# A GpSimd add behind each of 736 gathers in a four-layer sparse graph network

## The chip, the cores and the metric

The kernel runs on one core of a Trainium2 chip. The metric is device time in microseconds (us). Engines: PE is TensorE (matrix products; PEld its weight loads), DVE is VectorE, ACT is ScalarE, POOL is GpSimd, SP is SyncE, which only issues transfers here.

## What is computed

Four graph layers over 4096 nodes with 128 features each and one 4096x4096 weighted adjacency matrix, of which only a small part is not zero. Every layer normalises the rows, applies relu and adds its result to x:

```python
# layer 0
h = relu(layernorm(x)); x = x + h @ W_self.T + (adj @ h) @ W_neigh.T + b
# layer 1: three Chebyshev terms
h = relu(layernorm(x)); T1 = adj @ h; T2 = 2 * (adj @ T1) - h
x = x + h @ w[0] + T1 @ w[1] + T2 @ w[2] + bias
# layer 2: attention over the edges
H = h @ weight.T; C = alpha_src[None, :] + alpha_dst[:, None]
Tau = adj.T * exp(max(0.2 * C, C)); att = Tau / sum(Tau, axis=1)
x = x + (adj.T * att) @ H
# layer 3: one message for each edge
s = h @ msg_s; d = h @ msg_d
agg[i] = sum_j gelu(s[i] + d[j] + msg_b) * adj[i, j]
f = gelu(concat(h, agg) @ upd_w.T + upd_b) + h; x = x + layernorm(f)
```

The nodes are put in another order before the launch, so that nodes with many edges come first.

## The kernel before

The matrix is read once, half a block of 128 rows at a time (1 MB each), and turned into flags: ACT makes a mask of what is not zero (L768), DVE reduces it by columns (L783) and packs it into words (L788, L790), of which it takes the largest eight of each segment (L797). From the flags come lists. For each of 16 stripes of 256 rows, and likewise of columns, a list says which far rows of a block have an entry in the stripe at all; blocks near the diagonal and dense ones are taken whole. The lists are made in `pairs` (L627 to L675: small DVE instructions, and PE products with a selection matrix from `selection`, L619). For layer 3 every single edge is listed (`entries`, L805), 128 to a chunk, 158 chunks in all.

All that is listed is fetched by gathers: one indirect transfer on POOL's queue for 128 rows, by an index tile. They are issued by the helper `gather` (L552), so all have the line L553. By what they write and read:

- `rseg<-in_adjT` (68) and `cseg<-in_adj` (74): 256-column pieces of far matrix rows for the row and the column stripes. SP stores them in the tables `r_tab` and `c_tab` in HBM (L722), from which later layers read them as whole tiles `big`.
- `g<-h_tab` (136) and `g<-u_tab` (68): rows of the normalised features for layer 0 and for the first product of layer 1 (`h_tab`), and of layer 1's intermediate result for its second product (`u_tab`) (L1120).
- `g<-a_tab` (74): the same for attention (L1212).
- `e_val<-in_adj` (158): the matrix value of each edge (L937).
- `<-d_tab` (158): the rows d[j] of layer 3 (L1351), into tiles that the profile calls m, e or tau, as they share memory with attention's tiles of these names.

Other work on POOL: at the start tables of indices and constants, then xN + b0 for eight blocks at a time (L979, four of 128x1024), xN + b1 for four blocks (L1000, eight of 128x512), and four memsets (L1592). `pause` does not exist yet; `ones` (L445) is a 128x128 tile of ones that stays unchanged after L446.

The order on every engine is written by a planner in the kernel itself (class `Plan`, L255). Each piece of work is a generator that yields an engine with a planned duration, an event, or a pool of buffers; the planner always lets the piece start that can start earliest, and among those that could start at almost the same time the one with the lowest rank. A gather is planned with `GATHER`, 1.27 us on POOL. The value gathers (`values`, rank 6) and column pieces (rank 4) yield to the layers (rank 0). The result is kept: `in_order` (L348) ties each instruction to its predecessor on its engine. So each engine works through one fixed queue, and an instruction that waits holds up all behind it.

If PE has a planned gap of more than 0.8 us, `fill` (L604) puts products with a tile of zeros into it, one for each 0.22 us of 80% of the gap, into a free PSUM bank.

The Tile framework adds the waits on semaphores. A gather waits for its index tile, for the last reader of its buffer, and for the landing of the gather eight before it.

Of the kernel before, what the change touches and what calls it, by code (L numbers as in the profile page):

```python
# [27 lines left out]
P = 128  # L28
# [344 lines left out]


SP = "SP", 0.07
GATHER = "POOL", 1.27


def sparse_stack(tc, x, adj, adjT, diag, w_self, w_neigh, b0, w1, b1, w2, att_src, att_dst,
# [7 lines left out]
    nc = tc.nc  # L387
    plan = Plan()
    EARLY = 7
    with ExitStack() as ctx:  # L390
# [4 lines left out]
        def tiles(pool, name, n, shape, dtype=F32):  # L395
            return Slots([pool.tile(list(shape), dtype, name=f"{name}{i}", tag=f"{name}{i}") for i in range(n)])

        def kept(name, shape, dtype=F32):
            return keep.tile(list(shape), dtype, name=name, tag=name)
# [17 lines left out]
        banks = tiles(ps, "bank", 3, (P, BANK))  # L417
        picks = tiles(ps, "pick", 2, (P, BANK))
# [26 lines left out]
        ones = kept("ones", (P, P))  # L445
# [103 lines left out]
        junks = tiles(keep, "junk", 2, (P, D))  # L549
        aggs = tiles(keep, "agg", 2, (P, BANK))  # L550

        def gather(dst, table, index):  # L552
            nc.gpsimd.indirect_dma_start(out=dst, out_offset=None, in_=table[:, :],  # L553
                                         in_offset=bass.IndirectOffsetOnAxis(ap=index, axis=0))


        def norm(blocks, dst):
# [45 lines left out]

        def fill(begin, time):  # L604

            idle = min((free, i, slots.items) for slots in (banks, picks) for free, i in slots.free + [(1e9, 0)])
            if idle[0] < begin - 1.0:
                for _ in range(int(time / 0.22)):
                    nc.tensor.matmul(idle[2][idle[1]], nothing[:, :P], nothing, start=True, stop=True)  # L609
# [121 lines left out]
        def fetch_columns():  # L731
            for s in COLS:
                if s.cap:
                    yield col_list[s.index]
                for k in range(s.cap):
                    t = yield csegs
                    yield GATHER
                    gather(t, adj_segments, seg_col[:, s.chunk + k:s.chunk + k + 1])
                    here, left = Event(), Count(1)
                    here.set(plan.transfer(P * CS * 4))  # L740
                    plan.start(store(here, t, csegs, left, c_tab[s.index][k * P:(k + 1) * P, :], c_done[s.index],
                                     P * CS * 4), 6)
                    plan.start(give_back(left, csegs, t), 0)
# [186 lines left out]
        def values():  # L930
            for number, group in enumerate(GROUPS):
                yield decoded[number]
                for u in group.units:
                    for k in range(u.chunk, u.chunk + u.cap):
                        yield GATHER
                        n = u.within(k)
                        gather(e_val[:n, k:k + 1], adj_flat, e_at[:n, k:k + 1])  # L937
                        valued[u.number].set(plan.finish + plan.LANDING)
                    plan.start(valid(u), 7)
# [125 lines left out]
        class Layer:  # L1065
# [36 lines left out]
            def gather(self):  # L1102
                for s in ROWS:
                    if s.cap:
                        yield row_list[s.index]
                    for c in range(s.cap):
                        if self.number == 0:
                            t = yield rsegs
                            yield GATHER
                            gather(t, adjT_segments, seg_row[:, s.chunk + c:s.chunk + c + 1])  # L1110
                            here, left = Event(), Count(2)
                            here.set(plan.transfer(P * RS * 4))
                            self.at["seg", s.index, c] = t, here, left
                            plan.start(store(here, t, rsegs, left, r_tab[s.index][c * P:(c + 1) * P, :],
                                             r_done[s.index], P * RS * 4), 2)
                            plan.start(give_back(left, rsegs, t), 0)
                        g = yield rows_g
                        yield self.table_done
                        yield GATHER
                        gather(g[:, :D], self.table, fetch_row[:, s.chunk + c:s.chunk + c + 1])  # L1120
                        self.at["row", s.index, c] = g
                        self.rows_here[s.index][c].set(plan.transfer(P * D * 4))
# [51 lines left out]
        class Attention:  # L1174
# [33 lines left out]
            def rows(self, s, chunks, rows):  # L1208
                yield a_table
                for c, (g, here) in zip(chunks, rows):  # L1210
                    yield GATHER
                    gather(g, a_tab, fetch_col[:, s.chunk + c:s.chunk + c + 1])  # L1212
# [103 lines left out]
        class Messages:  # L1316
# [27 lines left out]
            def rows(self, u, chunks, m, here):  # L1344
# [3 lines left out]
                for q, k in enumerate(chunks):  # L1348
                    yield GATHER
                    n = u.within(k)  # L1350
# [300 lines left out]
def gnn_stack_kernel(tc, **args):  # L1651


    some_bad = sparse_stack(tc, **args)
    with tc.If(some_bad > 0):
        args.pop("diag")
        dense_stack(tc, **args)
# [329 lines left out]
```

## Time and profile before

| what | value |
|---|---|
| median of 9 runs | 1197.01 us (1193.78 to 1200.44) |
| the profiled execution, timed | 1198.3 us |
| its span, from first to last instruction | 1196.4 us |
| busy: PE / DVE / ACT / POOL | 988.1 / 797.7 / 673.1 / 769.3 us |
| mean granted PE clock | 0.921 |
| moved by DMA | 236.03 MB, mean 197 GB/s |
| e_val<-in_adj gathers | 158, mean 1011 ns |
| g<-h_tab gathers | 136, mean 980 ns |
| g<-a_tab gathers | 74, mean 1047 ns |
| zero products of fill (L609) | 795, 532 of them with mean 407 ns |
| chain that ended last | DMA 21%, PE 20%, DVE 12%, POOL 10%, issue 8%, ACT 6% |

The profile comes from one execution. Busy time counts instructions that an engine carries out; waiting, branches and the issue of plain transfers do not count. A gather counts as busy while POOL makes its descriptors, not while the data travel. Where one row of the profile joins several instructions, its duration runs from the first start to the last end. "issue" is time in which an engine waited for nothing that the profile shows.

Stages of this execution: reading, scanning, lists and layer 0 up to about 345 us; the rest of the column pieces, both products of layer 1, the features for attention and the decoding of the edges up to about 720; attention up to about 965; messages and the end up to 1196.

### The profile page before, as it was taken

To read this page: it belongs to the slowest core of one execution; us is meant where nothing else is said; L and a number is where in the kernel's file an instruction comes from. 1 tells how busy PE (TensorE), PEld (TensorE's weight loads), DVE (VectorE), ACT (ScalarE), POOL (GpSimd) and SP (SyncE) were. 2 spreads that over 40 slices of the span, in tenths; PEclk is the share of its full clock that TensorE was granted. 3 is DMA by queue.
4 is the path that set the end of the run, shared out by engine and by line. 5 is a ranking of instruction groups with operands and counts; after the bars stand their busy time and mean duration, and the time that the engine had idled before them with its cause. 6 is when DMAs were issued, how large, how long until landed. Compare 5 with 4: busy or idle time off the path is not lost.

```text
span 1196.4 us, 19187 instructions
## 1 busy us (share of the span) xinstructions
PE 988.1 (83%) x5943; PEld 678.6 (57%) x5943; DVE 797.7 (67%) x2982; ACT 673.1 (56%) x1344; POOL 769.3 (64%) x832
## 2 busy tenths in 40 slices
PE   5878989888888888878879798989999997879860
PEld 2545666555546666657767554454555655657650
DVE  5789988798788858758768575455555733456652
ACT  4997666677423121323456485676778632545771
POOL 5115777355466767777777777777777747777710
PEclk9988889888889999989999899999999999999985
DMA  7999999999659778899767433444445222233300
GB/s 225 372 329 346 387 390 395 373 334 374 197 159 301 217 217 272 272 269 277 226 177 211 136 89 111 115 113 115 115 127 144 68 59 53 51 75 79 78 22 21
DMA packets 175415, 236.03 MB, mean 197 GB/s; under 512 B 22452, under 2 KB 155336, under 8 KB 167112
## 3 DMA queue, kind: packets, MB, share of 16 engines
q1 hardware_dynamic: 148904, 186.45, 46.3%
q0 software_dynamic: 26400, 48.27, 16.1%
q8 instruction: 49, 0.80, 0.3%
q14 instruction: 62, 0.51, 0.1%
HBM read 203.41 MB, written 31.23 MB: 196 GB/s over the span
## 4 chain that ended last, share of the span: by engine, by line
DMA 21%; PE 20%; DVE 12%; POOL 10%; issue 8%; ACT 6%; SPq 0%; POOLq 0%; ACTq 0%; DVEq 0%
POOL e_val L553 4%; DMA e_val<-in_adj,e_at 4%; PE acc L1138 3%; DMA cseg<-in_adj,seg_col 3%; POOL g L553 3%; DMA g<-h_tab,fetch_row 3%; PE acc L1155 2%; DMA tau<-d_tab,e_col 2%; PE acc L1254 2%; PE acc L1252 2%; DMA g<-a_tab,fetch_col 2%; DMA big<-in_adjT 2%; DMA m<-d_tab,e_col 2%; DMA big<-r_tab 2%; PE bank L597 2%
## 5 line engine op out<-in xcount | busy, mean ns | idle before, releaser
L553 POOL DMA_INDIRECT e_val<-in_adj,e_at x158 | 159.7, 1011 | 48.0 <-issue 40.7
L553 POOL DMA_INDIRECT g<-h_tab,fetch_row x136 | 133.3, 980 | 44.7 <-issue 26.4
L609 PE MATMUL pick<-nothing 128*128 128x512 f16 x532 | 137.8, 407 | 0.0
L609 PEld LDWEIGHTS <-nothing 128*128 128x128 f16 x795 | 81.6, 105 | 90.8 <-issue 22.3
L1138 PE MATMUL acc<-big,hA 128*128 128x256 f32 x448 | 120.7, 415 | 6.9 <-DMA big<-in_adjT 4.8
L553 POOL DMA_INDIRECT rseg<-in_adjT,seg_row x68 | 70.0, 1030 | 75.0 <-issue 22.8
L1138 PEld LDWEIGHTS acc<-big,hA 128*128 128x128 f32 x448 | 89.2, 208 | 21.5 <-DMA big<-in_adjT 6.0
L553 POOL DMA_INDIRECT cseg<-in_adj,seg_col x74 | 71.4, 965 | 39.2 <-issue 20.5
L768 ACT ACTIVATE mask<-dst 128x2048 fp8e4<-128x2048 f32 x43 | 81.9, 1904 | 24.2 <-DMA dst<-in_adj 24.1
L553 POOL DMA_INDIRECT g<-a_tab,fetch_col x74 | 77.5, 1047 | 22.6 <-issue 14.6
L1155 PE MATMUL acc<-big,g 128*128 128x256 f32 x272 | 78.0, 421 | 16.4 <-DMA big<-r_tab 10.1
L553 POOL DMA_INDIRECT m<-d_tab,e_col x70 | 68.3, 975 | 21.3 <-issue 12.8
L553 POOL DMA_INDIRECT tau<-d_tab,e_col x63 | 61.2, 972 | 30.1 <-issue 11.6
L1235 DVE TENSOR_TENSOR tau<-e,big 128x512 f32<-128x512 f32 (+3 forms) x61 | 54.3, 890 | 39.3 <-ACT e L1231 37.1
L553 POOL DMA_INDIRECT g<-u_tab,fetch_row x68 | 64.9, 955 | 20.7 <-issue 10.1
L568 ACT ACTIVATE junk<-xN,stat 128x128 f32<-128x128 f32 x128 | 51.3, 401 | 40.0 <-DVE stat L564 29.5
L887 ACT COPY ehit<-pick 128x192 f32<-128x192 f32 (+7 forms) x74 | 20.3, 287 | 89.6 <-PE pick L884 70.7
L1155 PEld LDWEIGHTS acc<-big,g 128*128 128x128 f32 x272 | 52.8, 208 | 28.5 <-DMA g<-h_tab,fetch_row 10.4
L609 PE MATMUL bank<-nothing 128*128 128x512 f16 x263 | 68.3, 402 | 0.0
L1138 PE MATMUL acc<-big,hB 128*128 128x256 f32 x224 | 59.5, 403 | 7.7 <-DMA big<-in_adjT 7.7
L890 DVE SCALAR_TENSOR_TENSOR ehit<-ehit,pos,pick 128x32 f32<-128x32 f32 (+7 forms) x158 | 38.7, 284 | 38.0 <-ACT ehit L887 37.7
L622 ACT ACTIVATE sel_t<-iota_row,mids 128x512 f32<-128x512 f32 (+3 forms) x43 | 27.1, 642 | 57.7 <-DVE mids L617 55.7
(328 smaller groups left out, 2612.9 us busy)
## 6 DMA issues: line engine op xcount, KB each, us to landing
dst<-in_adj SPq DMA_DIRECT2D x43, 1024.0 KB, 9.6
big<-in_adjT SPq DMA_DIRECT2D x45, 512.0 KB, 7.3
raw<-in_adj SPq DMA_DIRECT2D x21, 1024.0 KB, 9.6
big<-in_adjT SPq DMA_DIRECT2D x66, 256.0 KB, 5.9
big<-r_tab SPq DMA_DIRECT2D x30, 512.0 KB, 6.1
c_tab<-cseg SPq DMA_DIRECT2D x74, 128.0 KB, 3.4
r_tab<-rseg SPq DMA_DIRECT2D x68, 128.0 KB, 8.8
big<-c_tab SPq DMA_DIRECT2D x15, 512.0 KB, 3.8
```

Of the source, the lines that this page charges most:

```text
L553: nc.gpsimd.indirect_dma_start(out=dst, out_offset=None, in_=table[:, :], in_offset=bass.IndirectOffsetOnAxis(ap=index, axis=0))
L568: nc.scalar.activation(junk, src[:, k, :], AF.Square, bias=st[:, 0, k:k + 1], accum_out=st[:, 1, k:k + 1])
L597: nc.tensor.matmul(p[:, k * D:(k + 1) * D], lhs[:, k * P:(k + 1) * P], w, start=i == 0, stop=i == len(terms) - 1)
L609: nc.tensor.matmul(idle[2][idle[1]], nothing[:, :P], nothing, start=True, stop=True)
L622: nc.scalar.activation(lane["t"][:, :n * P], iota_row[:, :n * P], AF.Abs, bias=mids[:, g:g + 1])
L768: nc.scalar.activation(mask[:, h * HALF:(h + 1) * HALF], raw_of[b, h], AF.Sigmoid, scale=1e38, accum_out=marks[:, 2 * b + h:2 * b + h + 1] ...
L890: nc.vector.scalar_tensor_tensor(hit[:, q, :], hit[:, q, :], pos0[:, k + q:k + q + 1], pv[:, q, W:2 * W], op0=ALU.is_le, op1=ALU.mult, acc ...
L1138: nc.tensor.matmul(acc, self.near[:, b, :D], as_rows(t)[:, k, :], start=count == 0, stop=count == every - 1)
L1155: nc.tensor.matmul(acc, row[:, :D], r, start=count == 0, stop=count == every - 1)
L1235: nc.vector.tensor_mul(tau[:, :n, :], e[:, :n, :], a[:, :n, :])
L1252: nc.tensor.matmul(acc[0:1, CS:2 * CS], parts[k][:, D + 1:], tau[:, k, :], start=False, stop=False)
L1254: nc.tensor.matmul(acc[:, :CS], parts[k][:, :D], e[:, k, :], start=False, stop=self.count[s.index] == every - 1)
```

## The change

Behind each indirect transfer, `gather` issues an elementwise add on POOL: `ones` plus `ones` into a new 128x128 f32 tile `pause`, which nothing reads. The planned duration of a gather goes from 1.27 to 1.52 us. In `fill`, the choice of an idle bank compares only time and number and no longer the lists of tiles when both are equal.

```diff
 SP = "SP", 0.07
-GATHER = "POOL", 1.27
+GATHER = "POOL", 1.52
...
+        pause = kept("pause", (P, P))
+
         def gather(dst, table, index):
+
             nc.gpsimd.indirect_dma_start(out=dst, out_offset=None, in_=table[:, :],
                                          in_offset=bass.IndirectOffsetOnAxis(ap=index, axis=0))
+            nc.gpsimd.tensor_add(pause, ones, ones)
...
         def fill(begin, time):
-            idle = min((free, i, slots.items) for slots in (banks, picks) for free, i in slots.free + [(1e9, 0)])
+            idle = min(((free, i, slots.items) for slots in (banks, picks) for free, i in slots.free + [(1e9, 0)]),
+                       key=lambda slot: slot[:2])
```

What is computed stays the same.

## The prediction

> **What bounds the kernel now.** I read the 40 slices first: two of the page's rows, busy tenths of the VectorE (DVE) and of GpSimd (POOL), each digit 29.9 us.
>
> ```profile
> DVE  5789988798788858758768575455555733456652
> POOL 5115777355466767777777777777777747777710
> ```
>
> From slice 14 on POOL stands at 7 almost throughout. A flat 7 is suspicious: a queue with slack shows holes. So I went to POOL's timeline; the columns are start, duration, instruction, and in brackets the idle time before it.
>
> ```profile
> 153.53 0.95 POOL L553 DMA_INDIRECT rseg<-in_adjT,seg_row  x1 [0.30 <-PE acc L1155]
> 154.50 1.28 POOL L1000 TENSOR_TENSOR xN<-xN,b_sb 128x512 f32<-128x512 f32 x1
> 155.93 0.97 POOL L553 DMA_INDIRECT g<-h_tab,fetch_row  x1 [0.16 <-issue]
> ```
>
> A gather takes 0.95 us and the next follows 0.30 us later, so back to back they come every 1.25 us, and 0.95/1.25 is the 7. Reading that timeline from end to end: the first of 736 gathers starts at 84.4, 157 start before 376, and from 376 to the last one nearly all gaps are those 0.30 us. The rest add up to 17.6 us: 6.4 us of column-segment waits before 526, and one wait of 11.2 us (10.9 beyond the normal gap).
>
> ```profile
> 967.73 0.95 POOL L553 DMA_INDIRECT tau<-d_tab,e_col  x1 [11.17 <-DMA d_tab<-agg]
> ...
> 1142.01 0.92 POOL L553 DMA_INDIRECT e<-d_tab,e_col  x1 [0.30 <-issue]
> ```
>
> So 579 gathers from 376 to 1143 hold POOL without pause: POOL sets the pace there, and the tail from 1143 to 1196.4 is what its last gathers feed. Before 376 it is another engine. By stages (columns: stage, its length, then busy us of PE, PE weight load, DVE, ACT, POOL, then PE clock, DMA share, GB/s):
>
> ```profile
> 84.00:201.00 117.00, 100.71 (x836) 72.25 (x837) 103.79 (x308) 84.71 (x127) 79.70 (x77) 0.90 1.02 376
> 201.00:345.00 144.00, 121.44 (x930) 78.38 (x929) 118.62 (x379) 87.69 (x133) 70.56 (x69) 0.86 0.87 308
> ...
> 376.00:720.00 344.00, 288.63 (x1611) 220.24 (x1610) 246.32 (x1326) 142.71 (x339) 256.90 (x267) 0.94 0.74 218
> 720.00:956.00 236.00, 216.33 (x971) 122.17 (x971) 129.72 (x254) 170.17 (x350) 182.81 (x180) 0.97 0.42 113
> 956.00:1143.00 187.00, 159.36 (x964) 119.74 (x964) 92.50 (x270) 90.49 (x188) 134.30 (x138) 0.95 0.27 65
> ```
>
> From 84 to 345 DVE is busy 222.4 of 261 us (scan of the matrix, row lists) and POOL only 150. There POOL waits in bursts, about 55 us beyond its gaps, for lists that DVE makes.
>
> **The change, part by part.**
>
> *The added instruction.* One 128x128 f32 add behind each gather: 736 in all, no transfer. No row has that shape, but two have the operation:
>
> ```profile
> L1000 POOL TENSOR_TENSOR xN<-xN,b_sb x8: 1261/1272/1283, 154.5 to 369.7; 128x512 f32<-128x512 f32 x8
> L979 POOL TENSOR_TENSOR xN<-xN,b_sb x4: 2352/2356/2803, 37.8 to 95.5; 128x1024 f32<-128x1024 f32 x4
> ```
>
> The line through 1.272 us at 512 and 2.356 us at 1024 elements has 2.12 ns per element and 0.19 us of start, which makes 0.46 us at 128. Bounds: below, the one-input select on 128x128 at L199 of masks.py, 0.29 us; above, 0.55 us, the 0.46 lengthened by 19% as the slowest L979 add was (2.80 against 2.36). I take 0.46, as the same operation outweighs the same shape.
>
> *What of it lies in the gap.* In the second fence above an add stands between gathers: it starts 0.02 us behind the gather, and the next gather 0.15 us behind it. Start to start that is 2.40 us where 1.26 is usual: an add of 1.28 us cost 1.14. The four memsets at 724 did the same (1.94 us, gap 0.16). So an add hides 0.14 us in the gap, and a pause costs POOL 0.32 us net (0.15 to 0.41 from the bounds). Its only wait is for the pause before it, a gather earlier, so that costs nothing while gathers are longer than adds; if it had to wait, 0.46 us would be added. Behind it on POOL stand the next gather, the bias adds and memsets. SP's stores of gathered segments wait for landings in order, and matrix loads stand behind them, so late gathers are passed on there too.
>
> *What it does to DVE.* This I did not expect to find. Whenever an add runs on POOL, some DVE instruction next to it is stretched until the add ends:
>
> ```profile
> 176.47 0.17 DVE L672 TENSOR_SCALAR prow<-prow 128x4 f32<-128x4 f32 x1
> 176.68 1.94 DVE L673 TENSOR_SCALAR seg_row<-prow 128x4 uint32<-128x4 f32 x1
> ...
> 197.13 1.90 DVE L670 TENSOR_TENSOR prow<-prow,pnone 128x4 f32<-128x4 f32 x1
> ```
>
> and POOL at those times:
>
> ```profile
> 176.35 0.94 POOL L553 DMA_INDIRECT g<-h_tab,fetch_row  x1 [0.30 <-issue]
> 177.31 1.27 POOL L1000 TENSOR_TENSOR xN<-xN,b_sb 128x512 f32<-128x512 f32 x1
> ...
> 197.74 1.27 POOL L1000 TENSOR_TENSOR xN<-xN,b_sb 128x512 f32<-128x512 f32 x1
> ```
>
> L673 is 0.17 us by its median, L670 0.16; here they take 1.94 and 1.90, ending with the add (178.58, 199.01). L779 at 226.18 and L668 at 369.18 do the same (1.95 and 1.86). They started 0.56 to 0.63 us before the add did, inside the gather in front, while neighbours that ended 0.64 us or more before the add, such as L672 here, were untouched. Ordinary gathers don't do this: L788, with two SBUF inputs, is 1.20 to 1.25 us in all 32. So an add behind a gather shuts out DVE's instructions of two SBUF inputs, and its tensor_scalar forms, from 0.61 us before its start to its end: 1.88 us for 512 columns, and 0.61 + 0.46 = 1.07 us for a pause, in a cycle of 1.25 + 0.32 = 1.57 us. Reductions and maxima pass (L783 keeps 1.22). The eight L1000 adds cost DVE 0.39, 1.77, 1.74, 1.77, 0.63, 0.93, 0 and 1.70 us: 1.12 on average, 0.6 of the time shut. A pause then costs DVE about 0.64 us. In the other direction an add waits for a running DVE instruction: L979 at 51.6 took 2.80 us behind L788.
>
> The Trainium skill (SBUF — State Buffer, "Who interferes with whom") says DVE and GpSimd share one port pair as an exclusive lock for the whole instruction, and that whoever starts first shuts the other out; that speaks against the change. By its words alone the lock would last the 0.46 us of the add, and the sum would stay near the POOL-only rival below; the rows show the extra 0.61 us, and they decide.
>
> *The planner.* The gather's planned cost goes from 1.27 to 1.52, so all orders are made anew. Comparing the two built programs: row, column and value gathers keep their numbers; among POOL's 748 gathers and other work the attention's gathers move ahead (median place 516 to 461), the last value gather falls back (585 to 604), the first message gather moves up (586 to 552). Nothing leaves POOL, so the total stays; the gain is that value gathers can fill the 10.9 us hole at 956, which I subtract. PE gets 396 more matmuls on the zero tile. At 0.215 us (the chain has six in 1.29) to 0.43 us (eleven in 4.69) that is 85 to 170 us, planned into time in which PE waits for gathers, so I cost it at nothing; on the path, without that cover, it would be those 85 to 170 us. The new sort key in fill only breaks ties.
>
> *The sum, stage by stage.* 84 to 345, 136 gathers: DVE 222.4 + 136 x 0.64 = 309 against 261: +48. 345 to 376, 20 gathers: 6 less 3.5 of idle: +3. 376 to 720, 267 gathers: POOL alone 344 + 85 - 6 = 423; DVE alone 246 + 171 = 417; the shared time, if the two never overlap, 267 x 1.07 + 181 = 467 (181 us is what DVE's instructions with SBUF inputs of those kinds add up to there). Two queues that both need the whole stage and exclude each other don't interlock perfectly, so I take the middle, 445: +101. 720 to 956, 175 gathers: POOL 236 + 56 = 292, shared 187 + 112 = 299, middle 296: +60. 956 to 1143, 137 gathers: POOL 187 + 44 - 11 = 220, shared 147 + 87 = 234, middle 227: +40. The tail has no gather: 0. Together +252 on the span of 1196.4: 1448. The profiled run was timed at 1198.3 and the median is 1197.0, so span and median differ by less than 1 us.
>
> **The rivals.**
>
> *POOL only.* DVE's losses are absorbed, because late lists only move POOL's idle time: 579 x 0.32 = 185, +8 before 376, -17 of holes: 1372. With the bounds 0.15 and 0.41 it gives 1274 and 1425. For it: POOL's idle 55 us before 345. Against: DVE has only 39 us free there, and its queue feeds the row lists.
>
> *DVE becomes the bound.* Each hold costs DVE its full 1.07 us: 222 + 146 = 368 (+107) before 345, 246 + 286 = 532 (+188) from 376 to 720, with +103 as before behind them: 1594. For it: four of eight adds cost almost the full hold. Against: the other four did not, and a quarter of DVE's work from 376 to 720 (246 less 181) passes.
>
> *The pause relieves the gathers: not slower.* Gathers above 0.945 us cost 35 us over the whole run (10, 6, 14 and 4 us in the four stages that begin at 84, 376, 720 and 956). If spacing made these all short and the 10.9 us hole closed, it would be 1150; it decides only if a pause costs POOL less than 46/579 = 0.08 us, an add of 0.22 us. Against: the select with one input takes 0.29.
>
> **How the numbers follow.** Shared port, 1400 to 1500: 0.58. POOL only, or a cheaper add, 1270 to 1400: 0.27. DVE as the bound, 1500 to 1620: 0.13. Not slower: 0.02. The time is the first one's, 1448; the range, 1350 to 1530, takes most of the second and the near part of the third. About 0.2% is what a measurement can tell from no change; faster 0.01, within it 0.01, slower 0.98.
>
> **What would show it.** In the profile after: pauses of about 0.46 us 0.02 us behind gathers, gathers every 1.57 us or more; POOL near 90% busy from about 430 on; the median of L673 or L1400 well above 0.17 and 0.34 us, and instructions of two SBUF inputs up to 1 us longer; L783 unchanged at 1.22. Layer 0 ending some 50 us later would confirm the first term. I am wrong if gathers follow each other every 1.3 us (the pause hides), if DVE rows keep their durations (POOL only), or if POOL shows long idle stretches behind DVE (the third).

## The result, and the profile after

| | before | after |
|---|---|---|
| median | 1197.01 us (31 runs, 1191.96 to 1206.5) | 1422.53 us (10 runs, 1418.52 to 1426.86) |
| ratio, 95% interval | | 1.1882 (1.1859 to 1.1905) |
| the profiled execution, timed | 1198.3 us | 1418.37 us |
| its span | 1196.4 us | 1416.5 us |
| busy PE / DVE / ACT / POOL | 988.1 / 797.7 / 673.1 / 769.3 us | 1116.5 / 890.2 / 673.1 / 1133.1 us |
| mean granted PE clock | 0.921 | 0.895 |

The change costs 18.8%: 225 us by the medians, 220 us in the span. In the changed kernel the gather is at L556 and the pause at L558; lines of the layers move by four or five. First the two rows of slices that the prediction began with, now 35.4 us a digit:

```profile
DVE  5899775898898887789875455454430033555642
POOL 4138988577888888888889989999988888888870
```

POOL's flat 7 has become a flat 8 and 9 from slice 10 on, while DVE falls to nothing in slices 30 and 31 (counted from 0): POOL is the bound, more plainly than before. The pauses as one group (columns: shapes and count, busy us, mean ns, idle us in front), then in POOL's timeline in the middle stage (start, duration, idle in front in brackets):

```profile
L558 POOL TENSOR_TENSOR pause<-ones 128x128 f32<-128x128 f32 x736 | 338.5, 460 | 13.9
```

```profile
561.14 0.41 POOL L558 TENSOR_TENSOR pause<-ones 128x128 f32<-128x128 f32 x1
561.70 0.96 POOL L556 DMA_INDIRECT e_val<-in_adj,e_at  x1 [0.16 <-issue]
562.68 0.41 POOL L558 TENSOR_TENSOR pause<-ones 128x128 f32<-128x128 f32 x1
563.25 0.96 POOL L556 DMA_INDIRECT cseg<-in_adj,seg_col  x1 [0.16 <-issue]
```

Gather to gather this is 1.55 us, against 1.25 before. A pause takes 0.41 us when nothing disturbs it and starts 0.02 us behind its gather; the mean of 0.460 us comes from some pauses that last longer. Of the 0.30 us gap, 0.14 us is hidden, as forecast: the net price is 0.295 us.

To compare stages I cut both runs at the same gathers: the first, and numbers 137, 157, 424, 599 and 735 counted from 0, which in the old run start at 84.4, 345.5, 376.5, 721.9, 967.7 and 1142.0, and in the new one at 83.6, 372.0, 407.3, 852.0, 1149.5 and 1372.6. Busy time by such stretches (columns as in the prediction's stage rows: stretch, length, then busy us of PE, PE weight load, DVE, ACT, POOL); of the kernel before, then of the one after:

```profile
84.00:345.50 261.50, 222.65 (x1767) 151.04 (x1767) 222.88 (x686) 172.39 (x259) 150.46 (x146) 0.88 0.94 338
...
376.50:722.00 345.50, 290.13 (x1616) 220.56 (x1616) 247.82 (x1327) 144.71 (x343) 258.56 (x268) 0.94 0.74 218
```

```profile
84.00:372.00 288.00, 232.81 (x1791) 151.86 (x1792) 235.30 (x690) 171.55 (x260) 223.81 (x283) 0.87 0.89 306
...
407.00:852.00 445.00, 366.83 (x1891) 262.02 (x1890) 331.90 (x1364) 184.76 (x421) 390.43 (x539) 0.91 0.64 188
```

The first pair is the reading that matters: 137 pauses added 73 us to POOL and only 12 us to DVE. The whole difference, put together from the starts and durations in POOL's timeline of both runs:

| from gather to gather | longer by | pauses x 0.295 | pauses beyond 0.412 | gathers longer | other work of POOL | remaining (idle of POOL) | forecast |
|---|---|---|---|---|---|---|---|
| 0 to 137 | 27.3 | 40.4 | 8.3 | 9.3 | 0 | -30.7 | 48 |
| 137 to 157 | 4.4 | 5.9 | 0.2 | -0.1 | 0 | -1.6 | 3 |
| 157 to 424 | 99.3 | 78.8 | 8.2 | 11.8 | 1.9 | -1.4 | 101 |
| 424 to 599 | 51.6 | 51.6 | 13.9 | 0.8 | -1.9 | -12.8 | 60 - 11 = 49 |
| 599 to 735 | 48.8 | 40.1 | 5.2 | 3.5 | 0 | 0 | 40 + 11 = 51 |
| behind the last gather | -10.4 | | | | | | 0 |

(The forecast took the hole of 10.9 us at 956 off its last term; cut by gathers it lies one row higher.) With the first gather 0.8 us earlier, the rows make the 220 us of the span. From gather 157 on, all that is left over is the hole that closed: the time is POOL's own pace, the pauses plus what lengthens POOL's instructions.

### The profile page after: what moved, and what is told of

Same layout as the page of the kernel before. It is cut to its first block, busy times and chain, and to the rows that moved or that the text cites. A ratio compares the mean times of both kernels' runs of the same rounds, so it can differ in the third digit from the quotient of the medians.

```text
span 1416.5 us, 20675 instructions
## 1 busy us (share of the span) xinstructions
PE 1116.5 (79%) x6339; PEld 735.4 (52%) x6339; DVE 890.2 (63%) x2982; ACT 673.1 (48%) x1343; POOL 1133.1 (80%) x1568
## 4 chain that ended last, share of the span: by engine, by line
POOL 33%; DVE 23%; PE 18%; DMA 11%; ACT 7%; issue 7%; POOLq 0%; SPq 0%; ACTq 0%; DVEq 0%
POOL pause L558 10%; POOL e_val L556 10%; POOL g L556 5%; POOL tau L556 3%; DMA g<-h_tab,fetch_row 3%; PE acc L1143 2%; POOL m L556 2%; PE acc L1160 2%; PE pick L614 2%; PE bank L601 2%; ACT mask L773 2%; ACT junk L572 2%; DMA m<-d_tab,e_col 1%; DMA raw<-in_adj 1%; PE bank L1411 1%
## 5 line engine op out<-in xcount | busy, mean ns | idle before, releaser
L558 POOL TENSOR_TENSOR pause<-ones 128x128 f32<-128x128 f32 x736 | 338.5, 460 | 13.9
L614 PEld LDWEIGHTS <-nothing 128*128 128x128 f16 x1191 | 123.5, 105 | 142.5 <-issue 33.5
L556 POOL DMA_INDIRECT e_val<-in_adj,e_at x158 | 167.5, 1060 | 24.9 <-issue 23.7
L556 POOL DMA_INDIRECT g<-h_tab,fetch_row x136 | 138.4, 1017 | 25.6 <-issue 15.3
L614 PE MATMUL bank<-nothing 128*128 128x512 f16 x641 | 153.4, 393 | 0.0
L614 PE MATMUL pick<-nothing 128*128 128x512 f16 x550 | 150.0, 423 | 0.0
L556 POOL DMA_INDIRECT rseg<-in_adjT,seg_row x68 | 75.7, 1114 | 38.6 <-issue 13.5
L950 DVE TENSOR_TENSOR e_val<-e_val,e_valid 128x3 f32<-128x3 f32 (+6 forms) x35 | 6.8, 195 | 151.4 <-DMA e_val<-in_adj,e_at 151.2
L556 POOL DMA_INDIRECT g<-a_tab,fetch_col x74 | 80.2, 1084 | 13.0 <-issue 9.8
L556 POOL DMA_INDIRECT tau<-d_tab,e_col x79 | 78.6, 994 | 12.4 <-issue 10.1
L556 POOL DMA_INDIRECT cseg<-in_adj,seg_col x74 | 71.7, 970 | 19.7 <-issue 10.6
L1240 DVE TENSOR_TENSOR tau<-e,big 128x512 f32<-128x512 f32 (+3 forms) x61 | 56.8, 930 | 48.8 <-ACT e L1236 46.4
L556 POOL DMA_INDIRECT g<-u_tab,fetch_row x68 | 65.5, 964 | 15.1 <-issue 9.5
L556 POOL DMA_INDIRECT m<-d_tab,e_col x67 | 67.0, 999 | 12.2 <-issue 7.7
L1160 PE MATMUL acc<-rseg,g 128*128 128x256 f32 x136 | 47.4, 450 | 27.9 <-DMA g<-h_tab,fetch_row 27.9
L1233 ACT ACTIVATE e<-dst,g 128x256 f32<-128x256 f32 x74 | 35.5, 501 | 66.4 <-DMA g<-a_tab,fetch_col 66.3
L1405 DVE TENSOR_SCALAR r<-iota_row,e_row,e_val 128x128 f32<-128x128 f32 x158 | 54.6, 419 | 19.3 <-PE acc L1423 9.0
```

The costliest lines, as they stand in the source:

```text
L558: nc.gpsimd.tensor_add(pause, ones, ones)
L1160: nc.tensor.matmul(acc, row[:, :D], r, start=count == 0, stop=count == every - 1)
L1233: nc.scalar.activation(e[:, k, :], dst[:, s.lo:s.lo + CS], AF.Relu, bias=h[:, D:D + 1])
L1240: nc.vector.tensor_mul(tau[:, :n, :], e[:, :n, :], a[:, :n, :])
L1405: nc.vector.tensor_scalar(r[:, q, :], iota_row[:, :P], e_row[:, k:k + 1], e_val[:, k:k + 1], op0=ALU.is_equal, op1=ALU.mult)
```

## What the experiments showed

Twelve kernels ran, in three groups of four, each group on one chip. On two of the three chips the kernel before took far longer than in the result above, and most expectations were reckoned from 1197 us. So every run stands beside the kernel before on its own chip ("orders of 1.52" or "1.27" are the instruction orders that the planner makes with that cost of a gather; all have the pause and 1.52 unless the edit says otherwise):

| label | edit | before on that chip | time | ratio (95%) |
|---|---|---|---|---|
| before_again | the kernel before | B: 1194.7 | 1197.0 | 1.0017 (0.9994 to 1.0041) |
| after_again | the kernel after | B | 1418.9 | 1.1862 (1.1817 to 1.1907) |
| late_only | no pause behind layer 0's 136 gathers | B | 1390.1 | 1.1646 (1.1595 to 1.1698) |
| memset2 | two f32 memsets for the add | B | 1556.5 | 1.3023 (1.2979 to 1.3066) |
| order_only | orders of 1.52, no pause | A: 1547.1 | 1616.0 | 1.0434 (1.0343 to 1.0525) |
| old_order | pauses, orders of 1.27 | A | 1440.3 | 0.9312 (0.9247 to 0.9377) |
| upper64 | add on partitions 64 to 127 | A | 2993.9 | 1.9331 (1.9205 to 1.9457) |
| lower32 | add on partitions 0 to 31 | A | 1412.1 | 0.9124 (0.9064 to 0.9184) |
| order_only2 | as order_only | C: 1497.0 | 1598.5 | 1.0735 (1.0644 to 1.0827) |
| cols8 | add on 8 columns | C | 1475.7 | 0.9883 (0.9797 to 0.9969) |
| memset400 | one 128x400 bf16 memset for the add | C | 1393.1 | 0.933 (0.925 to 0.9411) |
| early_old | orders of 1.27, pauses only at layer 0 | C | 1493.8 | 1.0012 (0.9945 to 1.008) |

On B the two kernels repeat their times. Times on A and C are not set against times on B.

### The early term: late_only

```diff
-            nc.gpsimd.tensor_add(pause, ones, ones)
+            if table is not adjT_segments and table is not h_tabs[0]:
+                nc.gpsimd.tensor_add(pause, ones, ones)
```

> No pause behind the 136 gathers of layer 0 (matrix pieces and rows), which POOL issues while the matrix is scanned; 600 remain. If DVE sets the pace there and the pauses stretch it (48 us forecast, 28 us measured at the last of them), the time falls by 25 to 50 us, to 1370 to 1395. If POOL catches up in its idle stretches there anyway: 1410 to 1425 us.

Without layer 0's pauses the kernel takes 28.8 us less than after_again. Gather number 140 starts at 347 us, against 380 in after_again and 353 in before_again. So the early term is some 28 us, near what the cut by gathers shows (27.3 + 4.4), and about 0.6 of the 51 us that were forecast. It is more than the 8 us that "POOL only" gave up to 376. Between gathers 0 and 137 of the kernel before, POOL's gaps above 0.4 us add up to 69 us beyond the usual 0.30 us each (the prediction has about 55), in 12 pieces. POOL gained 58 us of work: 31 us fell into these waits, 27 us did not. By the trace, ACT or PE ended 43 of the 69 us and DVE only 7, so "for lists that DVE makes" does not describe most of them.

The same run bears on the orders: it has those of 1.52, and without pauses in layer 0 it reaches gather 157 at 377 us, against 380 in before_again on the same chip. So up to there the new orders cost nothing on this chip, and behind it the table leaves no idle time of POOL in which a cost of theirs could lie.

early_old was to show the same term alone, with the old orders.

```diff
-GATHER = "POOL", 1.52
+GATHER = "POOL", 1.27
...
-            nc.gpsimd.tensor_add(pause, ones, ones)
+            if table is adjT_segments or table is h_tabs[0]:
+                nc.gpsimd.tensor_add(pause, ones, ones)
```

> The orders of before, with the pause behind the 136 gathers of layer 0 alone. If DVE and the lists set the pace of the scan and the pauses delay them, nothing behind it gives the delay back, as POOL is full from there to its last gather: 25 to 35 us more than before, 1220 to 1232 us. If POOL's idle stretches before 376 us take it up: at most 10 us more.

On chip C it can't be told from the kernel before. As that kernel takes 300 us more there for another reason (below), this says nothing of the early term: inconclusive.

### What holds DVE up, and when: lower32, memset400, cols8, memset2

What a pause does to DVE is seen well within one microsecond of the kernel after. DVE's timeline:

```profile
183.63 0.42 DVE L673 SCALAR_TENSOR_TENSOR prow<-at_row,at_block 128x4 f32<-128x4 f32 x1
...
184.62 0.51 DVE L677 TENSOR_SCALAR prow<-prow 128x4 f32<-128x4 f32 x1
```

and POOL's:

```profile
183.62 0.41 POOL L558 TENSOR_TENSOR pause<-ones 128x128 f32<-128x128 f32 x1
184.19 0.96 POOL L556 DMA_INDIRECT rseg<-in_adjT,seg_row  x1 [0.16 <-issue]
185.16 0.42 POOL L558 TENSOR_TENSOR pause<-ones 128x128 f32<-128x128 f32 x1
```

L673 (0.16 us when alone) starts with the first pause and ends with it. L677 (0.17 us when alone) starts 0.54 us ahead of the second pause, inside the gather, and ends at 185.13, 0.03 us before the profile shows that pause to begin. 311 DVE instructions that show alone in the timeline are lengthened by more than 0.08 us (the count shifts with the length that is taken as undisturbed); 140 of them start 0.45 to 0.75 us ahead of a pause, and 113 of these end by the time it starts, or within 0.12 us of that. So DVE is shut out twice, once inside the gather and once while the profile shows the pause, and gets through in between. The prediction had drawn one hold of 1.07 us from both.

lower32 leaves the part on partitions 32 to 127 out.

```diff
-            nc.gpsimd.tensor_add(pause, ones, ones)
+            nc.gpsimd.tensor_add(pause[:32, :], ones[:32, :], ones[:32, :])
```

> The pause adds only partitions 0 to 31. Both theories of the port agree that POOL pays 0.29 us per gather as before. If processors of the higher partitions took the port early, inside the gather, that lock is gone: no DVE instruction is stretched 0.4 to 0.7 us before a pause starts, pauses and gathers keep their undisturbed 0.41 and 0.95 us more often, and the time falls by 20 to 50 us, to 1370 to 1400. If POOL's time alone counts or the lock is one for all partitions: 1410 to 1430 us.

The lengthened DVE instructions fall from 311 (84 us) to 170 (43 us), and of the 140 that started 0.45 to 0.75 us ahead of a pause, 3 are left. Those that end with the pause stay (76 within 0.12 us, against 67). The early hold therefore comes from the add's share on partitions 32 to 127; that this share is worked off while the gather still runs is inferred from where the hold lies, and whether it matters that they are the upper ones was not shown. The Trainium skill (GPSIMD Engine Reference, "2.1 Instruction dispatch") says that each of GpSimd's cores serves 16 partitions and begins the next instruction as soon as its own share of the present one is done; that these 140 are gone agrees with it. On POOL nothing changes: pause mean 0.455 us, gather to gather 1.55 us. The kernel's 1412 us on chip A is no more than 11 us from the 1423 us of the kernel after on another chip. So the early hold is real, and it seems to cost little; a comparison across chips can't say more.

memset400 reads nothing, and holds POOL for the same time as the add.

```diff
-        pause = kept("pause", (P, P))
+        pause = kept("pause", (P, 400), BF16)
...
-            nc.gpsimd.tensor_add(pause, ones, ones)
+            nc.gpsimd.memset(pause, 1.0)
```

> In place of the add one memset of 128x400 (bf16), which reads nothing and by the memset rows (0.20 us at 128, 0.485 at 512 columns) takes 0.40 us, as long as an undisturbed add (0.41). If DVE and POOL shut each other out through what the add reads: DVE busy falls from 890 to some 800 us, the pauses and gathers keep their undisturbed lengths, and the time falls by 45 to 60 us against the changed kernel, to 1360 to 1375. If only POOL's time counts, or the lock is one for writes too: 1405 to 1425.

It took 1393 us, between the two expectations, on a chip of the other kind: as a time it decides nothing. The rows of DVE do decide something. The kernel after, a form with two SBUF inputs and one with scalars (last columns: busy us, mean ns, idle us):

```profile
L793 DVE TENSOR_TENSOR words<-mask,spread 128x1024 int32<-128x1024 int32 x32 | 41.1, 1283 | 0.0
...
L1405 DVE TENSOR_SCALAR r<-iota_row,e_row,e_val 128x128 f32<-128x128 f32 x158 | 54.6, 419 | 19.3 <-PE acc L1423 9.0 <-PE acc L1390 8.2 <-PE pick L1423 2.0
```

and with the memset:

```profile
L1405 DVE TENSOR_SCALAR r<-iota_row,e_row,e_val 128x128 f32<-128x128 f32 x158 | 56.4, 498 | 17.1 <-PE acc L1390 7.0 <-PE bank L1413 3.9 <-PE acc L1423 2.4
...
L793 DVE TENSOR_TENSOR words<-mask,spread 128x1024 int32<-128x1024 int32 x32 | 38.9, 1216 | 0.0
```

Before, these were 1217 and 350 ns. The memset leaves the two-input form alone and lengthens the scalar form even more than the add does (in cols8, on the same chip, it is 358 ns). The Trainium skill (SBUF — State Buffer, "Who interferes with whom") says that a DVE instruction with two SBUF inputs contends only with a GpSimd instruction that reads SBUF, while DVE's two-port modes, which tensor_scalar can enter, contend with GpSimd without that condition: both rows agree. DVE's reduction, L783 before and L788 now, which the prediction named as a form that passes, is 1221 ns before and after.

memset2 was to hold POOL as long with two f32 memsets.

```diff
-            nc.gpsimd.tensor_add(pause, ones, ones)
+            nc.gpsimd.memset(pause, 1.0)
+            nc.gpsimd.memset(pause, 2.0)
```

> In place of the add two memsets of 128x128, 0.20 us each, which read nothing: POOL is held as long as by the add. If DVE and POOL shut each other out through what the add reads, the stretched DVE instructions, pauses and gathers are mended, and the time falls by 40 to 60 us, to 1360 to 1385. If only POOL's time counts: 1405 to 1430 us.

As a test of equal length it failed, as its POOL timeline shows:

```profile
601.64 0.22 POOL L558 MEMSET pause<- 128x128 f32 x1
601.91 0.20 POOL L559 MEMSET pause<- 128x128 f32 x1
602.63 0.95 POOL L556 DMA_INDIRECT cseg<-in_adj,seg_col  x1 [0.52 <-issue]
```

The two memsets together are no longer than the add, but in front of 410 gathers the gap is above 0.4 us, as here, instead of 0.16; why was not found. That is a further point for POOL's pace: from gather 157 to the last the mean distance is 1.87 us, against 1.66 us in after_again on the same chip, and 0.21 us on 578 distances make 120 of the 132 us by which the span is longer. DVE's busy time is 804.3 us, near the 797.7 before: these memsets hardly slow DVE.

So the run also tells what the early stage hangs on. From gather 0 to gather 137, in before_again and in memset2 (columns as above):

```profile
83.90:349.00 265.10, 221.59 (x1767) 149.37 (x1767) 223.61 (x683) 171.84 (x259) 149.53 (x145) 0.89 0.93 333
```

```profile
84.50:384.30 299.80, 233.90 (x1808) 154.71 (x1809) 224.04 (x705) 173.26 (x262) 212.86 (x420) 0.87 0.86 295
```

DVE is as busy as before, and yet the stage is 35 us longer (28 us in after_again). What is put behind the gathers on POOL can lengthen it with no loss of DVE's; how much of the 28 us DVE's 12 us make was not separated. Why the f32 memsets spare the scalar form (r: 366 ns) and the bf16 one doesn't, is open; they differ in format and length at once.

cols8 makes the add short.

```diff
-            nc.gpsimd.tensor_add(pause, ones, ones)
+            nc.gpsimd.tensor_add(pause[:, :8], ones[:, :8], ones[:, :8])
```

> The add on 8 of the 128 columns. By the slope of the measured adds (2.1 ns per column, 0.41 us at 128) it takes 0.16 us, of which 0.14 hide in the gap: 0.02 to 0.05 us per gather on POOL, so 1200 to 1230 us on a chip where the kernel before takes 1195. If any instruction between two gathers costs a fixed 0.2 to 0.3 us, whatever its length: 1310 to 1370. If the pause is what keeps PE supplied on the other kind of chip, the time there is 1220 to 1300 us instead of 1547.

Its pause takes 0.21 us by the median, gathers follow each other every 1.35 us, and DVE's busy time is 802.6 us. It went 1.2% below the kernel before on chip C, which belongs to the next point.

### The orders, and a question left open: order_only, old_order, upper64, order_only2

```diff
             nc.gpsimd.indirect_dma_start(out=dst, out_offset=None, in_=table[:, :],
                                          in_offset=bass.IndirectOffsetOnAxis(ap=index, axis=0))
-            nc.gpsimd.tensor_add(pause, ones, ones)
```

> No pause; only the orders planned with 1.52 us for a gather, and the 396 additional zero products. If POOL's own time is what counts, its 736 gathers are the same as before, and the time is that of before, 1185 to 1210 us. If the new orders or the zero products do a good part of the harm, they cost 85 to 170 us here too: 1280 to 1370 us.

The other half of the change alone, the old orders with the pause:

```diff
-GATHER = "POOL", 1.52
+GATHER = "POOL", 1.27
```

> The pause behind each gather, but all orders planned with 1.27 us as before. If POOL's own time is what counts: 1400 to 1445 us, as with the changed kernel (1422). If the new orders do the harm: 1280 to 1330 us. If they repair a part of it: above 1445 us.

Both expectations were made for a kernel before of 1197 us, and it took 1547 us on that chip. So the share of the orders in the 225 us can't be taken from here, only from late_only above. order_only2 repeats the first of them on chip C:

> The new orders without the pause once more. On a chip where the kernel before takes 1195 us: 1185 to 1210 us if POOL's own time is what counts, since POOL has the same 736 gathers; 1240 us or more if the new orders themselves are worse, with PE in the 360 zero products that are planned into one hole at the start of the messages. On a chip where it takes 1547 us: 1600 to 1640 as before.

It is slower than the kernel before again, by 7.4%. On these chips the new orders without the pause cost 69 and 101 us, and the pause with the old orders saves 107 us (1547.1 - 1440.3). The last section shows where that time goes.

upper64 was to show whether a share on the upper partitions alone hides in the gather.

```diff
-            nc.gpsimd.tensor_add(pause, ones, ones)
+            nc.gpsimd.tensor_add(pause[64:, :], ones[64:, :], ones[64:, :])
```

> The pause adds only partitions 64 to 127 of the tiles (same 128 elements in each). If an instruction on POOL runs as one whole behind the gather, it lasts 0.41 us as before, gathers follow each other every 1.54 us, and the time stays near 1420 us. If a gather keeps only a part of POOL's processors busy, those of the low partitions, and the others already run the add during the gather, then the add hides: gathers every 1.25 to 1.35 us, 1195 to 1260 us, while DVE is still stretched inside the gathers.

It took 2994 us and answers another question, because with this form the pause waits until the gather in front of it has landed (last column: idle us in front of the pauses):

```profile
L558 POOL TENSOR_TENSOR pause<-ones 64x128 f32<-64x128 f32 x736 | 313.2, 426 | 1577.2 <-DMA g<-h_tab,fetch_row 357.5
```

What hides was not answered. What it does show is what a wait for the landing behind each gather would cost: 1577 us on POOL.

## Why the prediction was right, and where it was not

- *POOL sets the pace from gather 157 on.* Right: the remaining idle in the last three rows of the table is only the hole of 11 us and some 3 us more, and memset2 confirms it: a longer distance between gathers makes the kernel longer by nearly as much.
- *The pause: 0.46 us, 0.14 of it in the gap, 0.32 net.* Measured 0.412 undisturbed, 0.14 hidden, 0.295 net. The line through the two longer adds was 0.05 us too high for the bare add; that it met the mean (0.460) is chance, as this contains the lengthening.
- *84 to 345, +48.* The mis-sized term: +27.3. The step that failed is "A pause then costs DVE about 0.64 us". Cut by gathers, DVE gained 12.4 us on 137 pauses, 0.09 us each, and 92.5 us on all 736, 0.13 us each. The medians of L673 and L1400, which the prediction expected well above 0.17 and 0.34 us, stayed there (0.17 and 0.34 us at their new lines L678 and L1405). Two things were wrong in it. The hold of 1.07 us was taken as one piece, but it is two, with a way through between them. And the eight bias adds, from which the 0.6 came, are three times as long as a pause: a short hold probably falls more often between two DVE instructions, or on forms that pass (not shown by itself). The step from there to the time failed too: memset2 shows that POOL's own time lengthens this stage when DVE loses nothing. POOL's waits took up 31 us and 27 us were left. Up to gather 157 it is 32 us, where the sum had 51 and the POOL-only rival 8.
- *376 to 720, +101 as the middle of "POOL alone" and "shared port".* The sum was right (99.3), its make-up was not. POOL alone gives 79 us; the other 20 us are POOL's own instructions made longer, pauses by 8 and gathers by 12. DVE's 332 us in that stretch of 445 are far from the 417 us of the working.
- *The port.* That POOL pays is the direction to which the prediction gave one sentence and, but for its upper bound of 0.55 us, no price. Of the 76 pauses above 0.55 us, 39 overlap attention's additions at L1240 and L1242. DVE, then POOL, in the kernel after:

```profile
801.55 1.22 DVE L1240 TENSOR_TENSOR tau<-e,big 128x1024 f32<-128x1024 f32 x1
```

```profile
801.77 1.25 POOL L558 TENSOR_TENSOR pause<-ones 128x128 f32<-128x128 f32 x1
```

  DVE started 0.22 us earlier and kept its 1.22 us; the pause took 1.25 instead of 0.41.
- *720 to 956 and 956 to 1143.* 49 and 51 us forecast in the table's cut, 51.6 and 48.8 measured.
- *The tail, 0.* It became 10.4 us shorter: 44.0 us behind the start of the last gather, 54.4 before.
- *The planner's 396 extra products, 0.* Right on this kind of chip, by late_only and the table: 353 of them fill one hole (76 us from 1047.7), while POOL's digits stay at 8.
- *The rivals.* "POOL only" comes nearest in mechanism. Its 1372 us are 44 us below the span: 43 us by which pauses and gathers got longer behind gather 157 and 24 us more up to it, less 23 us by the smaller net price, the idle time and the tail. DVE did not become the bound. "The pause relieves the gathers" is wrong on this kind of chip: gathers got longer, from 0.993 to 1.028 us by the mean.

## What to carry to other kernels

When one queue runs back to back, price an instruction added to it by its duration less what fits into the gap, and add what the engines beside it do to it: here 0.295 us net became 0.37 us a gather (43 us of lengthening on 579 gathers). A lock seen beside a long instruction must not be scaled to a short one by its share of time; see first in which pieces the long one holds it, and which of its victims sit next to the short one. And run the baseline beside every experiment, on the same chip.

## What the hardware did that I had not expected

The kernel before took 1197 us on some chips, 1497 and 1547 us on others, and on those a pause of some 0.45 us behind every gather makes it faster (old_order, lower32, memset400). On chip C three kernels with the same orders differ only in what stands behind a gather: nothing (1598 us), 0.21 us (1476 us), 0.45 us (1393 us). More work on POOL, less time. POOL's slices of order_only2, then of memset400:

```profile
POOL 4144574455255655555634565567067115555610
```

```profile
POOL 4129999577788788888889989899988888888960
```

With nothing behind the gathers they still follow each other every 1.25 us, but in bursts: behind the first gather 29 waits above 5 us add up to 362 us (4 waits and 29 us in memset400). POOL waits for the others, and they wait for nothing that the profile shows: "issue" idle of PE, DVE and ACT is 156, 129 and 97 us in order_only2, 111, 88 and 82 in cols8, 18, 32 and 27 in memset400, and 0, 6 and 18 in the kernel before where it takes 1197 us. The plainest place is the hole that `fill` packs with zero products, which depend on nothing but their order. PE in order_only2, while gathers run back to back from 1156.15 to 1238.2:

```profile
1152.31 23.27 PE L613 MATMUL bank<-nothing 128*128 128x512 f16 x106
...
1195.51 0.58 PE L613 MATMUL bank<-nothing 128*128 128x512 f16 x1 [2.22 <-issue]
...
1206.71 0.58 PE L613 MATMUL bank<-nothing 128*128 128x512 f16 x1 [2.22 <-issue]
...
1248.00 12.19 PE L613 MATMUL bank<-nothing 128*128 128x512 f16 x45 [0.79 <-issue]
```

and in memset400, under gathers every 1.55 us:

```profile
1039.82 62.11 PE L614 MATMUL bank<-nothing 128*128 128x512 f16 x287
```

About 20 us into the burst, PE falls from a product every 0.22 us to one every 2.8 us, and comes back 10 us after the last gather. With 0.45 us behind each gather it does not fall in this hole. So on this chip PE issues far more slowly while gathers run back to back, and a pause relieves that. By which mechanism was not shown. The Trainium skill (Runtime: NRT & Kernel Launch, "Instruction fetch mechanics") says that each engine streams its instructions through a DMA queue of its own into a small buffer, at a cost that is mostly hidden. One might think that the gathers' transfers crowd out this queue until the buffer is empty. But the trace of order_only2 speaks against that. The queue q8 brings a block of 16 KB about every 256 instructions of PE; one block comes between 1168 and 1180 us and takes 0.95 us, and the next comes only at 1264. Of PE's products and weight loads, only about 100 start between the first block's end and 1244.5, where PE recovers. So if blocks are used in order, PE had instructions at hand all the while. Why some chips do it and others don't is open as well. The kernel after itself did not run on A or C; where old_order and lower32 gained 7% and 9% there, it would likely gain too.
